# A four-layer graph network on one core: constants of the radial filter loaded first, the first group's node work moved ahead of the edge compaction, and more turns for the last groups' convolutions in the closing steps

## The chip, the cores and the metric

The kernel runs on one core of one Trainium2 chip. The metric is the time of one execution on the device in microseconds. The kernel before took 1791.55 us, the median of three runs between 1784.43 and 1791.74 us. The profiled execution took 1791.61 us, and its page counts a span of 1789.7 us.

## What is computed

128 graphs of 64 nodes with 128 channels go through four layers. Each layer adds a graph operator to x and normalises the result over the channels. Cut to what matters here:

```python
# layer 0: continuous filter, 20 Gaussians of the distance, cosine cutoff at 5
f    = exp(-0.5 / widths**2 * (adj[..., None] - offsets)**2)
W    = (ssp(f @ fw1 + fb1) @ fw2 + fb2) * rcut(adj)[..., None]
agg  = einsum('bjf,bijf->bif', x @ w_in2f, W)
x    = layernorm(x + ssp(agg @ ow1 + ob1) @ ow2 + ob2)
# layer 1: the same form with 64 Gaussians, weighted by adj itself
g    = exp(coeff * (adj[..., None] - offsets1)**2)
Wf   = (ssp(g @ W1.T + b1) @ W2.T + b2) * adj[..., None]**2
y    = einsum('bjf,bijf->bif', x @ Wa.T, Wf)
x    = layernorm(x + ssp(y @ Wd1.T + bd1) @ Wd2.T + bd2)
# layer 2: two graph convolutions with D^-1/2 (A+I) D^-1/2 and elu; layer 3: one, with relu
x    = layernorm(x + gcn2(x, adj))
x    = layernorm(x + relu(norm(adj) @ x @ W.T + b))
```

`ssp` is softplus less log 2. About three quarters of the entries of `adj` are zero, and the kernel works on the nonzero ones only.

## The kernel before, in words

Two graphs make a pair: 128 rows on the 128 partitions, 64 pairs. The program has three parts.

**The opening** (lines 669 to 1674, up to the loop at line 1675). Vector (DVE) counts the edges of each node, and orders the nodes by their number of edges (`count`, `rank`). `permuted(s)` puts the adjacency rows of a set of eight pairs into that order: set 0 by matrix products and one store and two loads over DRAM (line 943, one half on the SP queue and one on the ACT queue), set 1 by eight indirect DMAs of GpSimd (POOL, line 910) and sixteen small loads (line 949). Then the constants of the layers are loaded over the ACT queue (lines 1144 to 1199): `neg_off`, `width` and `coeff` are the offset, the width and the factor of the Gaussians, each loaded in three copies of 20 rows, and Vector works on them (lines 1157 to 1160). `compact(0)` (line 1003) takes the largest entries of each row of set 0 by MAX8, FIND_INDEX8 and MATCH_REPLACE8 (lines 1033 to 1040), after POOL has cleared `comb` and `at` (lines 1017 and 1019); `pack` writes the packed distances d, column numbers j and cutoff weights w to DRAM. After that come a small filter for zero distance (lines 1208 to 1220), `loads(0)` and `loads(1)`, which read d, j and w of the first two pairs over the SP queue (line 1112), `node_before(0, 0)`, which makes the input features of the first group (four transposes, a copy `xt`, an addition on POOL at line 1304, four products, a copy `ys` on Scalar), and the first Gaussians (`gaussians`, line 1514).

**The loop.** 2 x 64 pair visits (layers 0 and 1), three chunks each, and two steps to drain: 386 steps, n and k being visit and chunk of step i. In a step the chunk of this step gets `filter_in` (product `px`, line 1542, and two Scalar passes `h`), the one before gets `gather` (product `pg`, line 1568, with the one-hot matrix `hot`, line 1527), and the one before that gets `filter_out` and `message` (products `pw`, line 1555, and two Vector products `m`, line 1583). After a pair's third chunk `slot_sums` reduces the messages to `agg` (lines 1606 and 1610), three reductions a step. Between these pieces the step gives turns to generators that do everything else: `nodes` (the node work after a group's sums, `node_after`), `befores`, `last`, and the two lanes `convs[0]` and `convs[1]`. A turn is one `next` of a generator, mostly one product into one of two PSUM banks (`ps_n`) or the work that reads it out; `slot` sees to it that a bank filled in one turn is read out in the next call. `graph_convs(q)` is layers 2 and 3 of group q in 29 turns; lane q % 2 takes it.

In layer 1 the groups are 0 to 14 of four pairs each, 15 of two pairs, and 16 and 17 of one pair. Groups 15 to 17 have their own queues in `last`, which get two turns a step. Everything that is still queued after the loop runs in rounds, one turn of each queue a round (the closing rounds).

**The order.** `in_order` ties the instructions of Vector and POOL to program order from the instruction `first` (line 668) to the loop, and those of all engines within the loop and after it. In the opening Scalar, TensorE and the DMA queues are ordered by the framework's scheduler; DMAs of the SP and ACT queues share eight completion semaphores in turn, and a DMA waits until the one before it on its semaphore has landed.

Of the kernel before, what the change touches and what calls it, by code (L numbers as in the profile page):

```python
# [11 lines left out]
F32 = mybir.dt.float32  # L12
AF = mybir.ActivationFunctionType
ALU = mybir.AluOpType
# [4 lines left out]
P = 128  # L19
# [561 lines left out]
def sparse_stack(ctx: ExitStack, tc: tile.TileContext, t: dict, out: bass.AP, flag):  # L581
# [85 lines left out]

    first = nc.cur_bb.bb.instructions[-1]


    places = [const.tile([NB, A], F32, name=f"place{i}") for i in range(2)]

# [3 lines left out]
    def run(queue, n):  # L676

        held = None
        while queue and n:
            try:  # L680
                held = next(queue[0])
                n -= 1
            except StopIteration:
                queue.popleft()
        return held
# [125 lines left out]
    def dram_ap(ap, offset, dims):  # L811
        return bass.AP(tensor=ap.tensor, offset=ap.offset + offset, ap=dims)
# [56 lines left out]
    def part(s):  # L869
        return slice(8 * s, 8 * (s + 1))  # L870

    def load_matrix(name, rows=C):
        w = const.tile([rows, C], F32, name=f"w_{name}")
        nc.scalar.dma_start(w, t[name])
        return w

    def column(name):
        return t[name].rearrange("(p o) -> p o", o=1)

    def load_column(name):  # L880
        b = const.tile([P, 1], F32, name=f"c_{name}")
        nc.scalar.dma_start(b, column(name))
        return b

    def load_terms(name):

        b = const.tile([1, C], F32, name=f"r_{name}")
        nc.scalar.dma_start(b, t[name].rearrange("(o p) -> o p", o=1))
        part_ = const.tile([1, 3, C], BF16, name=f"p_{name}")
        for i in range(3):  # L890
            nc.vector.tensor_copy(part_[:, i, :], b)
            if i < 2:
                nc.vector.tensor_sub(b, b, part_[:, i, :])
        terms = const.tile([3, GS, C], BF16, name=f"t_{name}")
        for s in range(GS):
            nc.scalar.dma_start(terms[:, s, :], part_[0:1].rearrange("o i c -> o (i c)"))
        return terms

    def load_rows(name):
        b = const.tile([P, C], F32, name=f"b_{name}")  # L900
        nc.scalar.dma_start(b, dram_ap(t[name], 0, [[0, P], [1, C]]))
        return b


    def big(name, n=640):
        return cpt.tile([P, 640], F32, tag="big", name=name, bufs=8)[:, 0:n]
# [189 lines left out]
        nc.tensor.matmul(u[0:1, 0:1], lhsT=odds, rhs=one, start=True, stop=True)  # L1096
        nc.vector.tensor_copy(flag, u[0:1, 0:1])

    def loads(n):


        layer, p = divmod(n, NP)
        size = GSLOTS[layer]
        s, at = p // 8, (p % 8) * 2 * size
        assert (layer, s) in stored, "slots are read before they are written"
        d = edge.tile([P, GSLOTS[1]], F32, tag="d", name=f"d_{n}", bufs=3)
        j = edge.tile([P, GSLOTS[1]], BF16, tag="j", name=f"j_{n}")
        w = edge.tile([P, GSLOTS[1]], F32, tag="w", name=f"w_{n}")

        def load(to, name, first, n):  # L1110

            nc.sync.dma_start(to, dram_ap(slots[layer, name][s], first, [[0, to.shape[0]], [1, n]]))  # L1112

        if layer == 0:
            third = 2 * size // 3
            for q in range(3):
                load(d[32 * q : 32 * (q + 1), 0:third], "d", at + q * third, third)
            d = d[0:96, 0:third]
        for b in range(2):
            rows, first = slice(A * b, A * (b + 1)), at + b * size  # L1120
            if layer == 1:
                load(d[rows, 0:size], "d", first, size)
            load(j[rows, 0:size], "j", first, size)
            load(w[rows, 0:size], "w", first, size)
        return d, j, w
# [7 lines left out]
    load_set(0)  # L1133
    permuted_rows, goes, hots = {}, {}, {}
    side, again0 = deque(), []

    goes_to(0)
    run(deque([permuted(0)]), -1)
    for s in (1, 2):
        load_set(s)  # L1140
    run(deque([permuted(1)]), -1)


    neg_off = [const.tile([P, 1], F32, name=f"neg_off{i}") for i in range(2)]
    coeff0 = const.tile([P, 1], F32, name="coeff0")
    width0 = const.tile([P, 1], F32, name="width0")

    fw1 = const.tile([P, C], F32, name="fw1")
    nc.gpsimd.memset(fw1, 0.0)
    nc.vector.memset(neg_off[0], 0.0)  # L1150
    nc.vector.memset(width0, 1.0)
    for q in range(3):
        at = slice(32 * q, 32 * q + NG0)
        nc.scalar.dma_start(fw1[at, :], t["L0_gnn_fw1"])
        nc.scalar.dma_start(width0[at, :], column("L0_gnn_widths"))
        nc.scalar.dma_start(neg_off[0][at, :], column("L0_gnn_offsets"))
    nc.vector.tensor_mul(width0, width0, width0)
    nc.vector.reciprocal(coeff0, width0)
    nc.vector.tensor_scalar(coeff0, coeff0, -0.5, None, ALU.mult)
    nc.vector.tensor_scalar(neg_off[0], neg_off[0], -1.0, None, ALU.mult)  # L1160

    off1 = offsets1()
    width1 = np.float32(off1[1] - off1[0])
# [35 lines left out]
    g["b0"], g["b1"] = load_column("L2_gnn_b0"), load_column("L2_gnn_b1")  # L1199
    g["b2"] = load_rows("L2_gnn_b2")  # L1200
    g["W3"] = load_matrix("L3_gnn_WT")
    g["b3"] = load_terms("L3_gnn_b")
    run(deque([compact(0)]), -1)

    w = layers[0]
    g0 = const.tile([P, 1], F32, name="g0")
    nc.vector.memset(g0, 0.0)
    act(g0[0:32], g0[0:32], AF.Square, bias=neg_off[0][0:32])  # L1210
    act(g0[0:32], g0[0:32], AF.Exp, scale=coeff0[0:32])
    u = ps_n.tile([P, 512], F32, tag="n", name="zero_x")
    nc.tensor.matmul(u[:, 0:1], lhsT=fw1[0:32, :], rhs=g0[0:32], start=True, stop=True)
    h0 = const.tile([P, 1], F32, name="h0")
    act(h0, u[:, 0:1], AF.Exp, bias=w["b1"])
    act(h0, h0, AF.Ln, scale=0.5, bias=half)
    u = ps_n.tile([P, 512], F32, tag="n", name="zero_w")
    nc.tensor.matmul(u[:, 0:1], lhsT=w["w2"], rhs=h0, start=True, stop=True)
    zero_filter = const.tile([P, 1], F32, name="zero_filter")
    nc.vector.tensor_add(zero_filter, u[:, 0:1], w["b2"])  # L1220

    def late_constants():


        eye = const.tile([P, A], F32, name="eye")
        nc.vector.tensor_add(eye, ident[:, 0:A], ident[:, A : 2 * A])
        deg = const.tile([P, NP], F32, name="deg")
        for s in range(NS):
            part_ = a_all[:, part(s), 0:A]
            yield from wait_steps(PACE - 2)  # L1230
            nc.vector.tensor_add(part_, part_, eye.unsqueeze(1).to_broadcast([P, 8, A]))
            yield
            nc.vector.tensor_reduce(deg[:, part(s)], part_, AX.X, ALU.add)
            yield
        g["dinv2"] = const.tile([P, NP], F32, name="dinv2")
        g["dinv3"] = const.tile([P, NP], F32, name="dinv3")
        some = const.tile([P, NP], F32, name="some")

        nc.vector.tensor_scalar(some, deg, 0.0, None, ALU.is_gt)
        nc.vector.tensor_scalar(g["dinv2"], deg, TINY, None, ALU.max)  # L1240
        nc.vector.tensor_scalar(g["dinv3"], deg, GCN_EPS, None, ALU.add)
        for i in (2, 3):
            dinv = g[f"dinv{i}"]
            for s in range(NS):
                yield from wait_steps(PACE)
                nc.gpsimd.tensor_tensor(dinv[:, part(s)], dinv[:, part(s)], neg_half[:, 0:8], ALU.pow)
        yield from wait_steps(PACE)
        nc.vector.tensor_mul(g["dinv2"], g["dinv2"], some)

# [39 lines left out]
    def node_before(layer, q):  # L1291

        w = layers[layer]
        name = f"{layer}_{q}"
        xs = x_all[:, GROUPS[layer][q], :]
        n = xs.shape[1]
        flat, ps = bank(f"xT_{name}", n)
        for s in range(n):
            nc.tensor.transpose(ps[:, s, :], xs[:, s, :], ident)
        yield True  # L1300
        xt = node.tile([P, 512], F32, tag="xt", name=f"xt_{name}", bufs=1)[:, 0 : n * P]
        nc.vector.tensor_copy(xt, flat)

        nc.gpsimd.tensor_tensor(xs, xs, w["c2"].unsqueeze(1).to_broadcast([P, n, C]), ALU.add)
        yield
        flat, ps = bank(f"y_{name}", n)
        for s in range(n):
            nc.tensor.matmul(  # L1308
                ps[:, s, :], lhsT=xt[:, s * P : (s + 1) * P], rhs=w["win"], start=True, stop=True
            )  # L1310
        yield True
        y = node.tile([P, n, C], F32, tag=f"y{n}", name=f"ys_{name}", bufs={GS: 3, 2: 1, 1: 2}[n])
        act(y, ps, AF.Copy)
        feats[layer, q] = y
        yield

    zblk = const.tile([P, GS, P], F32, name="zblk")
    nc.gpsimd.memset(zblk, 0.0)
# [318 lines left out]
        yield from late_constants()  # L1637

    N = 2 * NP
    for n in range(2):  # L1640
        slot_data[n] = loads(n)
    run(deque([node_before(0, 0)]), -1)
    gaussians(0, 0)
    gaussians(0, 1)
    one_hot(0)
# [29 lines left out]
    for i in range(3 * N + 2):  # L1675
# [15 lines left out]
        if n < N:  # L1691
# [14 lines left out]
                    one_hot(n)  # L1706
            filter_in(c)
        slot(nodes)
        if k == 1 and befores:
            slot(befores)  # L1710
        for queue in last:
# [66 lines left out]
```

## Time and profile before

| part of the span | what the profile shows |
|---|---|
| 0 to 78 us | the opening; TensorE has 9.3 us of work in the first 80 us, Vector 54.5 us |
| 78 to 1728 us | the loop; TensorE and Vector both near nine tenths busy |
| 1728 to 1783 us | the closing rounds |
| whole span | TensorE 1574.4 us busy (88%), Vector 1568.2 (88%), Scalar 1402.2 (78%), POOL 622.7 (35%) |

A line of the timeline has the start in us, the duration, the engine (a `q` after its name is its queue of DMAs), the line of the kernel, the operation, what it writes and reads, and in brackets how long the engine had been idle and what ended that. A line of the stretches view has the start and end of a stretch, its length, then the busy time of TensorE, of its weight loads, of Vector, Scalar and POOL with the number of instructions, then the granted share of the TensorE clock and the use of DMA.

### The profile page before, as it was taken

To read this page: it belongs to the slowest core of one execution; us is meant where nothing else is said; L and a number is where in the kernel's file an instruction comes from. 1 tells how busy PE (TensorE), PEld (TensorE's weight loads), DVE (VectorE), ACT (ScalarE), POOL (GpSimd) and SP (SyncE) were. 2 spreads that over 40 slices of the span, in tenths; PEclk is the share of its full clock that TensorE was granted. 3 is DMA by queue.
4 is the path that set the end of the run, shared out by engine and by line. 5 is a ranking of instruction groups with operands and counts; after the bars stand their busy time and mean duration, and the time that the engine had idled before them with its cause. 6 is when DMAs were issued, how large, how long until landed. Compare 5 with 4: busy or idle time off the path is not lost.

```text
span 1789.7 us, 23999 instructions
## 1 busy us (share of the span) xinstructions
PE 1574.4 (88%) x6806; PEld 786.9 (44%) x6806; DVE 1568.2 (88%) x4457; ACT 1402.2 (78%) x1680; POOL 622.7 (35%) x934
## 2 busy tenths in 40 slices
PE   1298989898989998999999999999999999999975
PEld 1133434444444444444444445454454544545443
DVE  7599989999989998879788999899998898988984
ACT  1277878788878887888999888888888888888840
POOL 2134353525333233214312333234242243332345
PEclk9999999999989998999999999999999999999995
DMA  5354545455445444534655655555555555545400
GB/s 140 89 121 120 148 128 129 112 123 130 120 117 124 104 119 105 128 97 119 148 135 123 143 122 122 136 118 128 123 134 126 119 123 132 125 118 132 96 7 15
DMA packets 123463, 210.12 MB, mean 117 GB/s; under 512 B 44709, under 2 KB 71478, under 8 KB 123318
## 3 DMA queue, kind: packets, MB, share of 16 engines
q1 hardware_dynamic: 114112, 202.18, 47.5%
q0 software_dynamic: 4352, 5.02, 1.0%
q10 hardware_dynamic: 4854, 1.27, 0.3%
q8 instruction: 56, 0.92, 0.2%
q14 instruction: 89, 0.73, 0.2%
HBM read 195.87 MB, written 12.51 MB: 116 GB/s over the span
## 4 chain that ended last, share of the span: by engine, by line
PE 43%; DVE 31%; DMA 7%; ACT 6%; issue 6%; SPq 3%; POOL 3%; DVEq 0%; ACTq 0%; POOLq 0%
PE pw L1555 16%; PE pg L1568 8%; PE px L1542 7%; DVE m L1583 6%; DVE agg L1606 6%; DVE hot L1527 5%; ACT h L830 2%; DMA cb<-code_dram 2%; SPq L1112 2%; DVE st L1276 2%; DMA d<-d_dram 2%; DVE mv L1277 2%; ACT g L830 2%; PE y L1308 1%; PE o L1387 1%
## 5 line engine op out<-in xcount | busy, mean ns | idle before, releaser
L830 ACT ACTIVATE g<-pg 128x728 f32<-128x728 f32 (+1 forms) x384 | 313.0, 815 | 163.4 <-PE pg L1568 156.7
L830 ACT ACTIVATE h<-h,half 128x728 f32<-128x728 f32 (+2 forms) x385 | 364.6, 947 | 12.5
L1568 PE MATMUL pg<-hot,ys 64*128 64x364 f32 (+1 forms) x1536 | 363.8, 551 | 0.1
L1606 DVE TENSOR_REDUCE agg<-m 128x16 f32<-128x288 f32 (+9 forms) x896 | 342.3, 430 | 2.1
L1281 POOL TENSOR_TENSOR rs<-rs,neg_half 128x4 f32<-128x4 f32 (+2 forms) x70 | 68.7, 981 | 736.6 <-DVE rs L1279 730.6
L1555 PE MATMUL pw<-h,w_L_gnn_fw 128*128 128x364 f32 x768 | 294.7, 509 | 31.7 <-DVE m L1583 31.7
L1555 PE MATMUL pw<-h,w_L_gnn_W2T 128*128 128x420 f32 x768 | 315.5, 533 | 3.2 <-DVE m L1583 3.2
L1583 DVE SCALAR_TENSOR_TENSOR m<-pw,c_L_gnn_b,g 128x420 f32<-128x420 f32 x384 | 239.9, 650 | 50.9 <-PE pw L1555 35.1
L1583 DVE SCALAR_TENSOR_TENSOR m<-pw,c_L_gnn_fb,g 128x364 f32<-128x364 f32 x384 | 212.1, 589 | 39.9 <-PE pw L1555 36.3
L830 ACT ACTIVATE h<-px,c_L_gnn_b 128x840 f32<-128x840 f32 x192 | 183.5, 956 | 60.2 <-PE px L1542 60.2
L1568 PEld LDWEIGHTS pg<-hot,ys 64*128 64x128 f32 x1536 | 118.2, 189 | 192.9 <-ACT h L830 107.3
L1555 PEld LDWEIGHTS pw<-h,w_L_gnn_fw 128*128 128x128 f32 x768 | 138.0, 198 | 137.8 <-DVE m L1583 73.7
L1555 PEld LDWEIGHTS pw<-h,w_L_gnn_W2T 128*128 128x128 f32 x768 | 130.6, 190 | 140.7 <-issue 76.2
L1527 DVE SCALAR_TENSOR_TENSOR hot<-j,row,w 128x1092 f32<-128x1092 bf16 (+1 forms) x128 | 183.4, 1432 | 5.1 <-DMA w<-w_dram 5.1
L1542 PE MATMUL px<-d,fw 32*128 32x364 f32 x768 | 173.0, 527 | 14.5 <-ACT h L830 12.1
L830 ACT ACTIVATE h<-px,c_L_gnn_fb 128x728 f32<-128x728 f32 x192 | 165.8, 864 | 11.2 <-PE px L1542 7.3
L1542 PE MATMUL px<-d,w1t 64*128 64x420 f32 x768 | 174.4, 531 | 0.0
L830 ACT ACTIVATE d<-d,neg_off 96x728 f32<-96x728 f32 (+1 forms) x128 | 141.8, 1108 | 0.0
L910 POOL DMA_INDIRECT rows<-comb,goes x64 | 68.4, 1069 | 141.7 <-DMA rows<-comb,goes 90.5
L1542 PEld LDWEIGHTS px<-d,fw 32*128 32x128 f32 x768 | 58.7, 186 | 117.0 <-ACT h L830 49.4
L1283 POOL TENSOR_SCALAR x_all<-ny,mv,rs 128x128 f32<-128x128 f32 x128 | 100.8, 797 | 3.6
L1542 PEld LDWEIGHTS px<-d,w1t 64*128 64x128 f32 x768 | 68.5, 186 | 53.3 <-issue 38.2
(219 smaller groups left out, 2135.0 us busy)
## 6 DMA issues: line engine op xcount, KB each, us to landing
d<-d_dram SPq DMA_DIRECT2D x128, 315.0 KB
w<-w_dram SPq DMA_DIRECT2D x128, 315.0 KB
w<-w_dram SPq DMA_DIRECT2D x128, 273.0 KB
j<-j_dram SPq DMA_DIRECT2D x128, 157.5 KB
d<-d_dram SPq DMA_DIRECT2D x192, 91.0 KB
j<-j_dram SPq DMA_DIRECT2D x128, 136.5 KB
x_all<-in_x_dram SPq DMA_DIRECT2D x8, 512.0 KB
cb<-code_dram SPq DMA_DIRECT2D x31, 128.0 KB
```

What stands on the lines that cost most here:

```text
L830: latest = nc.scalar.activation(out_, in_, func, **kw)
L910: nc.gpsimd.indirect_dma_start(out=into, out_offset=bass.IndirectOffsetOnAxis(ap=at, axis=0), in_=rows, in_offset=None,)
L1112: nc.sync.dma_start(to, dram_ap(slots[layer, name][s], first, [[0, to.shape[0]], [1, n]]))
L1276: nc.vector.bn_stats(stats[:, s, :], y[:, s, :])
L1281: nc.gpsimd.tensor_tensor(rstd, rstd, neg_half[:, 0:n], ALU.pow)
L1283: nc.gpsimd.tensor_scalar(dst[:, s, :], y[:, s, :], mv[:, s, 0:1], rstd[:, s : s + 1], ALU.subtract, ALU.mult,)
L1527: nc.vector.scalar_tensor_tensor(hots[n][:, 0:size], j[:, 0:size], near, wt[:, 0:size], ALU.is_equal, ALU.mult)
L1542: nc.tensor.matmul(ps[:, b, 0:n], lhsT=w["w1"][rows, :], rhs=d[rows, col : col + n], start=True, stop=True,)
L1555: nc.tensor.matmul(ps[:, 0 : c["size"]], lhsT=c["w"]["w2"], rhs=c["h"][:, b, :], start=True, stop=True)
L1568: nc.tensor.matmul(ps[:, b, 0:n], lhsT=y[rows, :], rhs=hots[c["n"]][rows, at], start=True, stop=True,)
L1583: nc.vector.scalar_tensor_tensor(messages[n][:, b, at], c["pw"][b][:, 0:size], c["w"]["b2"], c["g"][:, b, :], ALU.add, ALU.mult,)
L1606: nc.vector.tensor_reduce(av[:, :, :, r], both, AX.X, ALU.add)
```

## The change

The changed kernel has three edits. It moves what the Gaussians need (`neg_off`, `coeff`, `width`, `fw1`) from behind `permuted(1)` to directly behind `first`, so that their loads and the Vector work on them come first. It puts the other constants' loads ahead of `goes_to(0)`, moves the zero filter and `node_before(0, 0)` ahead of `compact(0)`, issues the three d loads of the first pair from the ACT queue, and takes `load_terms` (a bias in three bf16 terms, five small Vector operations and four DMAs) into the late constants inside the loop. And in the last steps (i of 372 and above) each step gives one more turn to each of the two lanes of convolutions, so that groups 12, 13 and 14 get further before the closing rounds.

```diff
+    neg_off = [const.tile([P, 1], F32, name=f"neg_off{i}") for i in range(2)]
+    coeff0 = const.tile([P, 1], F32, name="coeff0")
+    width0 = const.tile([P, 1], F32, name="width0")
+
+    fw1 = const.tile([P, C], F32, name="fw1")
+    nc.gpsimd.memset(fw1, 0.0)
+    nc.vector.memset(neg_off[0], 0.0)
+    nc.vector.memset(width0, 1.0)
+    for q in range(3):
+        at = slice(32 * q, 32 * q + NG0)
+        nc.scalar.dma_start(fw1[at, :], t["L0_gnn_fw1"])
+        nc.scalar.dma_start(width0[at, :], column("L0_gnn_widths"))
+        nc.scalar.dma_start(neg_off[0][at, :], column("L0_gnn_offsets"))
+    nc.vector.tensor_mul(width0, width0, width0)
+    nc.vector.reciprocal(coeff0, width0)
+    nc.vector.tensor_scalar(coeff0, coeff0, -0.5, None, ALU.mult)
+    nc.vector.tensor_scalar(neg_off[0], neg_off[0], -1.0, None, ALU.mult)
...
-    def loads(n):
+    def loads(n, engine=nc.sync):
...
-            nc.sync.dma_start(to, dram_ap(slots[layer, name][s], first, [[0, to.shape[0]], [1, n]]))
+            (engine if name == "d" else nc.sync).dma_start(to, dram_ap(slots[layer, name][s], first, [[0, to.shape[0]], [1, n]]))
...
-    goes_to(0)
-    run(deque([permuted(0)]), -1)
-    for s in (1, 2):
-        load_set(s)
-    run(deque([permuted(1)]), -1)
...
-    g["b3"] = load_terms("L3_gnn_b")
-    run(deque([compact(0)]), -1)
-
+    goes_to(0)
+    run(deque([permuted(0)]), -1)
+    for s in (1, 2):
+        load_set(s)
+    run(deque([permuted(1)]), -1)
...
     nc.tensor.matmul(u[:, 0:1], lhsT=w["w2"], rhs=h0, start=True, stop=True)
+
+    run(deque([node_before(0, 0)]), -1)
+    run(deque([compact(0)]), -1)
     zero_filter = const.tile([P, 1], F32, name="zero_filter")
...
     def late_constants():
 
+        yield from load_terms("L3_gnn_b")
...
-    for n in range(2):
-        slot_data[n] = loads(n)
-    run(deque([node_before(0, 0)]), -1)
+    slot_data[0] = loads(0, nc.scalar)
+    slot_data[1] = loads(1)
...
         slot(nodes)
+        if i >= 3 * (N - GS):
+
+            slot(convs[0])
+            slot(convs[1])
         if k == 1 and befores:
```

The helpers `load_matrix`, `column`, `load_column`, `load_terms`, `load_rows`, and `bank` to `node_before`, move with them; `load_terms` becomes a generator and issues its four DMAs from the SP queue.

## The prediction

> **What bounds the kernel now.** I read the stretches first, to see which engine the loop, its last steps and the closing rounds wait for; then Vector's waits in the first 100 us; then the opening in the timeline, with the chain of waits for the landings; then the closing rounds in the timeline.
>
> Stretches (start and end, length, busy time and number of instructions of TensorE, its weight loads, Vector, Scalar and POOL, granted clock, DMA share, GB/s): steady loop, the last 14 steps, the closing rounds.
>
> ```profile
> 1600.00:1660.00 60.00, 58.10 (x261) 30.04 (x260) 54.32 (x129) 52.50 (x60) 21.62 (x27) 1.00 0.57 132
> 1660.00:1728.00 68.00, 61.59 (x266) 31.28 (x265) 59.96 (x137) 49.45 (x61) 26.36 (x34) 0.99 0.21 49
> 1728.00:1784.00 56.00, 34.01 (x150) 25.62 (x148) 36.26 (x127) 5.31 (x15) 31.93 (x48) 0.68 0.05 14
> ```
>
> TensorE is 97% busy in the steady loop, 91% in the last 14 steps (Vector 88%), and 61% in the closing rounds, where the clock falls. So nothing in the steady loop is for sale; the change can act on the opening, on those 14 steps, and on the closing rounds.
>
> Vector's longest wait in the first 100 us, and the opening around it:
>
> ```profile
> DVE neg_off L1160 <- DMA neg_off<-in_L_gnn_offsets_dram: 8.7, 1, 8.7
> ```
>
> ```profile
> 4.72 0.69 DVE L770 TENSOR_SCALAR within<-entries 128x1024 bf16<-128x1024 f32 x1 [1.81 <-DMA entries<-in_adj_dram]
> ...
> 11.24 1.23 DVE L697 TENSOR_TENSOR halves<-some 128x2048 bf16<-128x2048 bf16 x1
> ...
> 39.88 0.69 SPq L943 DMA_DIRECT2D ad<-perm  x1
> ...
> 43.84 0.96 POOL L910 DMA_INDIRECT perm<-a_all,index  x1 [0.30 <-issue]
> ...
> 46.14 0.65 ACTq L943 DMA_DIRECT2D ad<-perm  x1
> ...
> 49.22 0.15 DVE L1160 TENSOR_SCALAR neg_off<-neg_off 128x1 f32<-128x1 f32 x1 [8.69 <-DMA neg_off<-in_L_gnn_offsets_dram]
> ...
> 51.78 1.11 DVE L1033 MAX8 comb<-ad 128x8 f32<-128x64 f32 x8
> ...
> 75.36 1.27 POOL L1304 TENSOR_TENSOR x_all<-x_all,b_L_gnn_ob 128x512 f32<-128x512 f32 x1 [4.43 <-PE xT L1299]
> ...
> 78.17 0.60 ACT L830 ACTIVATE ys<-y 128x512 f32<-128x512 f32 x1 [4.49 <-PE y L1308]
> 78.67 0.89 ACT L830 ACTIVATE d<-d,neg_off 96x728 f32<-96x728 f32 x1
> ...
> 80.54 1.58 PE L1542 MATMUL px<-d,fw 32*128 32x364 f32 x4 [2.40 <-ACT d L830]
> ```
>
> The ACT queue holds, in order, three loads of `fw1`, the second half of `ad`, and the last `neg_off`. The first waits for the memset of `fw1`, which stands on POOL behind eight indirect DMAs (the last from 43.84). So half of `ad` leaves at 46.14, though SP's half left at 39.88, and Vector stands until 49.22. At the other end of the opening, `ys` is on Scalar ahead of the first Gaussians.
>
> The chain of waits (start, duration, what) shows what a load costs here, among the entries' megabytes and in quiet:
>
> ```profile
> 1.38 4.78 DMA b<-in_L_gnn_fb_dram
> 6.18 3.70 DMA entries<-in_adj_dram
> ...
> 46.83 2.29 DMA neg_off<-in_L_gnn_offsets_dram
> ```
>
> The closing rounds:
>
> ```profile
> 1727.19 0.65 DVE L1583 SCALAR_TENSOR_TENSOR m<-pw,c_L_gnn_b,g 128x420 f32<-128x420 f32 x1 [0.35 <-PE pw L1555]
> ...
> 1734.99 0.49 PE L1367 MATMUL u<-agg,w_L_gnn_Wd1T 128*128 128x128 f32 x2 [3.44 <-DVE gz L1506]
> ...
> 1746.63 1.93 PE L1456 MATMUL hw<-w_L_gnn_W,er 128*128 128x128 f32 x8 [0.95 <-DVE er L1414]
> ```
>
> After the last `m` (end 1727.84) the last pair, group 17, still needs its node work and its 29 turns; its `u` starts at 1734.99, behind reductions and groups 13 and 14.
>
> [...] 4.78 us for a bias among the entries, 2.29 us for `neg_off` in quiet. [...] the 8.69 us at line 1160 hold the compaction queued behind it. [...] 0.68 granted in the closing rounds, and the eight products `hw` there take 1.93 us against 1.16 us in the loop (at 1701.65).
>
> **The change part by part.**
>
> *Constants first.* The built order of the changed kernel puts Vector's work on `width0`, `coeff0` and `neg_off` at the head, ahead of the counting, which Vector starts at 4.72 now. It waits for six small loads. The third `width` load is held until the load of `w` has landed (3.05), the third `neg_off` load until the bias `b` has (1.38 + 4.78 = 6.16); it then lands after 2.29 us in quiet (8.5) or 3.7 us behind an entries load (9.9). I take 3.0: 9.2. Behind this wait on Vector is all of the counting. From there: 0.15 for `neg_off`, about 0.8 of small work now done before 4.7, then four pairs of passes at 0.645 us each pass without gaps, 5.15. `halves` starts at 15.3 instead of 11.24: Δ = 4.0 (3.3 to 4.7; 2.6 if the load is back by 7.9). Scalar's `below` pass and the other constants' loads lie beside this.
>
> What it buys: `fw1` is no longer between the halves of `ad`, so both leave at about 39.9 + Δ and land some 3 us later. But POOL's order is now eight indirect DMAs (end 44.8 + Δ), the addition on `x_all` (1.27), the memset of `comb` (0.39): the first MAX8 can start at 46.5 + Δ. Gain: 51.78 − 46.5 − 4.0 = 1.3 us (0.6 to 2.7). The terms of the bias (1.2 us on Vector, 49.29 to 50.55) are within this; in the loop they are five short instructions among 386 steps, and I count nothing: they can go into the 10% that Vector idles.
>
> *Node work and zero filter ahead of compaction; d over the ACT queue.* Scalar ends the cosine at 70.47, loads a table (1.28) until 71.8, and can issue the d loads at once, where SP issued them at 72.71: 0.9 us. Landing 3.2 us after issue, as now (72.71 to 75.88), at 75.0. Then two Gaussian passes (0.9 each): `px` at 76.9 instead of 80.54, 3.6 us sooner, for `xT`, `y` and `ys` are done by then. Not all of it stays: the second d load and the first `hot` (ready about 82 on this scale) hold the steps after. I take 2.8 (2.0 to 3.6). The node work itself, 1.1 + 0.7 + 2.1 + 0.6 us on three engines, lies in the 40 us in which TensorE does next to nothing; the addition on POOL is counted above.
>
> Opening: −1.3 − 2.8 ≈ −4 (−2 to −5.5).
>
> *Two more turns a step.* In the built order 13 of Vector's instructions move from behind the last `m` to before it: group 13's end (`gy_sup` 0.69, `gz` 0.60, four statistics with their aggregates and `rs`, 1.7) and five turns of group 14 (`er` 0.6, `gy_hw` 0.6): 4.2 us. On TensorE group 13's `sup` 1.1 and `o` 1.4 and group 14's `hw` 1.1: 3.6; on POOL 4.5, which has room. If the 14 steps keep TensorE at 61.6/68 busy, they grow by 3.6/0.906 = 4.0; by Vector's measure 4.2/0.88 = 4.8. I take 4.4. From both sides: nothing, if the turns go into the 6.4 and 8 us of idle time; 7.5 if I walk through the new order with today's durations, because earlier turns put products right behind the Vector work they read: group 13's `gh` behind `gxt`, which is behind a `hot` (2.5), group 14's `u` behind its sums (1), group 15's `u` behind two groups' statistics (3), with 1 us more of small ones.
>
> What the closing rounds give back: group 17's chain sets their end, and the removed work is only partly on it. Its `u` starts 7.15 us after the last `m` now and would at 6.3, for a statistics block of group 13 stands ahead of it; after that fewer turns share the engines for the first rounds. The walk gives 53.6 us from the last `m` to the last normalisation against 55.5: −2 (−0.5 to −5; 5 would be all the moved work of TensorE at half clock, 1.7 + 1.6 + 1.6).
>
> End: +4.4 − 2 = +2.4. Whole: −4 + 2.4 = −1.6: 1790 us.
>
> **The rivals.**
>
> A, both ends fill: the moved turns cost nothing in the 14 steps, since the stretch before them shows that 97% can be had, the rounds give all 5 back, and the opening gives 5.5: 1791.55 − 10.5 = 1781. Against it: in these steps Vector too is at 88%, and in-order queues make waits of added turns.
>
> B, the last steps stall: the walk is right, +7.5, the rounds return only 0.5, the opening 2: +5, 1797 us, slower. For it: the wait of 3.44 us at group 17's `u` shows such a wait behind a reduction already. Against: the walk adds up waits that the real order may overlap.
>
> C, the wait moves from the middle to the head: each late `neg_off` load queues behind a megabyte, comes at 12 to 13, Δ reaches 7.5, and the first MAX8 comes 2.2 later than now; with 2.8 back at the end of the opening this leaves −0.6 of the 4: with +2.4, 1793 us, slower by little. For it: the bias of 4.78 us. Against: the entries are gone by 9.9.
>
> **How the numbers follow.** Forecast 0.52, A 0.25, B 0.16, C 0.07. The predicted time is the forecast's 1790. The range reaches to A and B with a little more for the runs' own spread (7 us between the three before): 1778 to 1799. Faster by over 0.5% is below 1782.6: most of A and the forecast's lower edge, 0.24. Slower by over 0.5% is above 1800.5: B's edge, and a spread that falls badly, 0.12. The rest, 0.64, cannot be told from no change.
>
> **What would show it right or wrong.** Right: Vector's wait at its head ends at about 9.2 and `halves` starts near 15.3; the first MAX8 starts near 50.5, released by the memset of `comb` on POOL; the first `px` near 75.6 instead of 80.54; from there the loop runs as now to step 372; the 14 steps from the first of them to the last `m` take some 4 us more, with TensorE's added idle time behind `gxt`, `agg` or the statistics; from the last `m` to the end some 2 us less. Wrong: a head wait over 12 us; a first step that starts early but is given back by a later wait for d, j or the edges; 14 steps of the same length or over 6 us longer; closing rounds that fall by 5, or not at all.

## The result, and the profile after

The changed kernel takes 1799.42 us (median, 1797.76 to 1801.56), the kernel before 1790.25 us in the same comparison (1784.43 to 1791.74). The ratio is 1.0058, 95% interval 1.0032 to 1.0084: slower by 9 to 10 us, where 1790 us were predicted. The profiled executions differ by 6.1 us (spans 1795.8 and 1789.7 us), and the traces show where.

To find the place I read from each trace the end of certain message products (the 768 instructions that write `m`, two a step): the first, the 385th (start of layer 1), the 737th (step 370, just ahead of the last steps) and the last one.

| end of message product, us | before | after | difference |
|---|---|---|---|
| 1st | 91.10 | 87.18 | −3.92 |
| 385th | 870.10 | 862.08 | −8.02 |
| 737th | 1656.46 | 1648.44 | −8.02 |
| 768th, the last | 1727.85 | 1734.54 | +6.69 |
| end of the span | 1789.7 | 1795.8 | +6.1 |

The changed kernel is 4 us ahead when the loop begins and 8 us when its last steps begin; those lose 14.7 us, and the closing rounds return 0.6. In what follows, "last steps" is the stretch from the end of the 737th message product to the end of the last one, and "closing rounds" the stretch from there to the end.

**The opening.** Vector's waits in the first 100 us, and the timeline of the changed kernel:

```profile
DVE hot L1531 <- DMA w<-w_dram: 8.9, 1, 8.9
DVE width L719 <- DMA width<-in_L_gnn_widths_dram: 6.1, 1, 6.1
...
DVE neg_off L722 <- DMA c_L_gnn_fb<-in_L_gnn_fb_dram: 2.5, 1, 2.5
```

```profile
10.14 0.15 DVE L722 TENSOR_SCALAR neg_off<-neg_off 128x1 f32<-128x1 f32 x1 [2.47 <-DMA c_L_gnn_fb<-in_L_gnn_fb_dram]
...
15.70 1.23 DVE L751 TENSOR_TENSOR halves<-some 128x2048 bf16<-128x2048 bf16 x1
...
51.54 1.11 DVE L1055 MAX8 comb<-ad 128x8 f32<-128x64 f32 x8 [1.87 <-POOL comb L1039]
...
76.58 1.65 PE L1546 MATMUL px<-d,fw 32*128 32x364 f32 x4 [29.03 <-ACT d L884]
```

The wait of 8.7 us for `neg_off` in the middle is gone; two waits at Vector's head (6.1 and 2.5 us) have come, until 10.14. `halves` starts 4.5 us later than before, yet the first MAX8 0.2 us sooner and the first `px` 4.0 us sooner (80.54 before). The MAX8 is released by POOL's memset of `comb`. For the second wait at the head the profile names a load that `neg_off` doesn't read; what the operation needs by the code is its own last load, issued at 6.20, 3.9 us before. (Such a wait of one load for the landing of another is in the trace of before: SP's last load of `entries` stood 4.1 us until the ACT queue's `b` had landed, which it doesn't read.) The longest wait in the list, of the first `hot` for its weights w, ends at 80.20 (81.13 before); the product `pg`, which reads `hot`, starts at 81.75.

**The last steps and the closing rounds.** The two stretches, the kernel before first, then the changed one.

```profile
1656.46:1727.85 71.39, 64.98 (x281) 32.53 (x278) 63.11 (x150) 52.95 (x65) 28.60 (x36) 0.99 0.25 58
1727.85:1789.72 61.87, 34.16 (x150) 25.77 (x149) 36.41 (x127) 5.31 (x15) 31.93 (x48) 0.67 0.05 15
```

```profile
1648.44:1734.54 86.10, 71.73 (x305) 36.88 (x301) 68.26 (x163) 53.05 (x65) 37.48 (x41) 0.94 0.22 51
1734.54:1795.84 61.30, 29.78 (x125) 22.02 (x124) 32.48 (x114) 5.20 (x15) 26.82 (x43) 0.66 0.04 11
```

TensorE gets 6.75 us more busy time. By the prediction's count 3.6 of them are the moved products; the rest, about 3 us, is my estimate for the lower granted clock (0.94 against 0.99). Its idle time grows from 71.39 − 64.98 = 6.4 us to 86.10 − 71.73 = 14.4. What TensorE waits for in that stretch, before and after (total, times, longest):

```profile
PE u L1367 <- DVE agg L1610: 3.7, 2, 2.6
PE back L1396 <- DVE gxt L1469: 1.1, 1, 1.1
```

```profile
PE u L1371 <- DVE agg L1614: 6.0, 3, 3.6
PE gh L1477 <- DVE gxt L1473: 4.6, 2, 2.6
PE y L1263 <- DVE nh L1379: 1.5, 1, 1.5
```

Not all of these waits are new. The three of `u` in the changed kernel are those of groups 14 (1.10 us), 15 (3.58) and 16 (1.32); before, group 14's was 1.04, group 15's nothing and group 16's 2.62. `y` doesn't read `nh`. By the code it takes the PSUM bank of `u`, which `nh` reads out, so that wait is for a bank.

The product `gh` of group 13 in the kernel before, then the first of the new waits in the timeline of the changed kernel, and the piece of the stretch in which that `gh` runs:

```profile
1664.37 1.12 PE L1473 MATMUL gh<-gxt,w_L_gnn_W 128*128 128x512 f32 x2 [0.23 <-DVE gxt L1469]
```

```profile
1654.17 1.52 DVE L1531 SCALAR_TENSOR_TENSOR hot<-j,row,w 128x1260 f32<-128x1260 bf16 x1
...
1655.61 0.69 DVE L1473 COPY gxt<-gx 128x512 f32<-128x512 f32 x1
...
1656.35 2.08 PE L1477 MATMUL gh<-gxt,w_L_gnn_W 128*128 128x512 f32 x2 [2.60 <-DVE gxt L1473]
...
1658.21 2.06 PE L1559 MATMUL pw<-h,w_L_gnn_W2T 128*128 128x420 f32 x4
1659.68 1.29 DVE L1587 SCALAR_TENSOR_TENSOR m<-pw,c_L_gnn_b,g 128x420 f32<-128x420 f32 x2 [2.79 <-PE pw L1559]
```

```profile
1655.78:1659.19 3.41, 2.84 (x4) 1.45 (x5) 1.11 (x2) 0.68 (x1) 3.02 (x4) 0.50 0.63 149
```

The product `gh` of group 13 waits 2.60 us for its copy `gxt`, which is behind `hot` on Vector. `pw`, queued behind `gh`, comes late, and then Vector stands 2.79 us for `pw`. `gh` takes 2.08 us, where the same product took 1.12 before: the granted clock is 0.50 there. In the last steps the trace has the clock at 1.00 except for three such pieces of 3.41 us (from 1655.78, 1720.63 and 1730.87); before, only the final 1.56 us of the stretch lie in one. Each of the three begins during or within 1 us after a wait of TensorE (2.60, 2.04 and 1.32 us). The longest wait, 3.58 us until 1712.11, is followed by none.

### The profile page after: what moved, and what is told of

It is laid out like the page before. It is cut to its first block, busy times and chain, and to the rows that moved or that the text cites. A ratio compares the mean times of both kernels' runs of the same rounds, so it can differ in the third digit from the quotient of the medians.

```text
span 1795.8 us, 24007 instructions
## 1 busy us (share of the span) xinstructions
PE 1572.4 (88%) x6806; PEld 787.1 (44%) x6806; DVE 1569.0 (87%) x4457; ACT 1402.2 (78%) x1681; POOL 624.6 (35%) x934
## 4 chain that ended last, share of the span: by engine, by line
PE 42%; DVE 34%; DMA 7%; ACT 7%; issue 5%; SPq 3%; POOL 2%; DVEq 0%; ACTq 0%; POOLq 0%
PE pw L1559 15%; PE pg L1572 8%; DVE m L1587 7%; PE px L1546 7%; DVE agg L1610 6%; DVE hot L1531 5%; ACT h L884 2%; SPq L1134 2%; DVE st L1231 2%; DVE mv L1232 2%; DMA d<-d_dram 2%; ACT g L884 2%; DMA cb<-code_dram 2%; DVE at L1058 1%; PE o L1391 1%
## 5 line engine op out<-in xcount | busy, mean ns | idle before, releaser
L884 ACT ACTIVATE h<-px,c_L_gnn_b 128x840 f32<-128x840 f32 x192 | 183.4, 955 | 58.5 <-PE px L1546 58.5
```

What stands on the lines that cost most here:

```text
L884: latest = nc.scalar.activation(out_, in_, func, **kw)
```

## The experiments

The kernels below ran on four chips, each time together with the kernel before, whose median there was 1792.4, 1802.8, 1802.2 and 1790.9 us in turn; so across chips only ratios to the kernel before are compared. Each stretch comes from one profiled execution. From the 385th to the 737th message product nearly every kernel below takes 786.3 to 786.4 us (one takes 785.1), so what is before and after it can be read apart.

**Each end of the change alone.** `open_only` is the changed kernel without these lines, `end_only` the kernel before with them:

```diff
         slot(nodes)
+        if i >= 3 * (N - GS):
+            slot(convs[0])
+            slot(convs[1])
```

> The changed kernel without the extra turns in the last steps. The traces show the changed kernel 3.9 us ahead after the first message product and 8.0 us ahead before the last steps. Theory 1 (the opening is a real gain, and the last steps alone lose): the last 14 steps and the closing rounds are as in the kernel before, so 1790.25 - 8.0 = 1782 us. Rival (only the 4 us of the opening are caused by the change, the other 4 are chance of one execution): 1786 us. The prediction on record put the opening at -4: 1786 us.

> The kernel before with the two extra turns a step alone. Theory 1 (the loss is in the last steps and has nothing to do with the opening): 71.4 us from the first of the last steps to the last message product become 86 us, the closing rounds give 0.6 back: 1790.25 + 14 = 1804 us. The prediction on record, taken alone: +2.4, 1793 us. Rival (the loss needs the changed opening, by another phase of the queues): at most 1795 us.

Measured: `open_only` 0.9986 of before (0.9976 to 0.9997), 2.5 us less by the ratio; `end_only` 1.0098 (1.0074 to 1.0122), 17.5 us more. The last steps of `open_only`, then of `end_only`:

```profile
1651.34:1723.52 72.18, 65.77 (x280) 32.84 (x278) 63.11 (x149) 52.92 (x65) 28.52 (x36) 0.98 0.25 57
```

```profile
1653.42:1740.02 86.60, 71.59 (x304) 36.71 (x301) 68.33 (x162) 52.92 (x65) 37.66 (x41) 0.94 0.22 51
```

So the loss is the third edit's alone and needs nothing of the opening.

The opening gains some 2 to 6 us up to layer 1 in single profiles; the 8 us of the first profile were partly chance. Kernels on the same chip show it: the 385th message product ended at 867.0 us with the old opening (`end_only`) and at 865.0 and 865.2 with the new one; on the second chip at 878.5 with the old one and at 873.3 and 873.9 with the new; on the third at 878.3 and 878.5 with the old one and at 872.4 with the new. The 1782 us of theory 1 failed; 2.5 us are nearer to the 4 of its rival and of the prediction, which the interval just includes.

**Place.** The same turns at the end of the step, or at its head ahead of `hot`:

```diff
         run(side, 1)
+        if i >= 3 * (N - GS):        # turns_at_step_head
+            slot(convs[0])
+            slot(convs[1])
...
         for queue in last:
             slot(queue)
+        if i >= 3 * (N - GS):        # turns_at_step_end
+            slot(convs[0])
+            slot(convs[1])
         past = [c, c1]
```

> The changed kernel with the same two extra turns in the same steps, moved from behind the node turn (ahead of filter_out) to the end of the step. Theory P (place: the turns put a convolution product right behind the Vector copy it reads and ahead of the ready products pw, so TensorE stands with pw queued behind it): no wait of gh on gxt of 2.6 us in these steps, they grow by about 5 us instead of 14.7, total 1782 + 5 = 1787 us (1784 to 1791). Theory W (amount: there is no room on Vector and TensorE in these steps, wherever the turns stand): 1799 us, as the changed kernel.

> The changed opening with both extra turns at the head of the step, before the one-hot matrix is put on Vector's queue. It takes away the cause of the longest single wait of the changed kernel (product gh of group 13 behind the copy gxt, which stands behind hot, 2.6 us) without taking a turn away. Theory C (turns there cost wherever they stand, since Vector and TensorE wait for each other in turn): that wait goes and others come, the last steps still take 84 to 89 us. Rival (this one order is bad): at most 80 us.

Measured: 1.0088 (1.0071 to 1.0105) at the end, 1.0034 (1.0020 to 1.0048) at the head; last steps 88.6 and 86.4 us. My theory of the place fell: at the end of the step the wait of `gh` shrinks (1.0 us in all), but `u` waits 10.8 us for `agg`, and `sup` 3.4 for `nTs`. At the head `gxt` does stand ahead of `hot`, and `gh` still waits 2.21 us for it, behind messages and sums on a Vector that is never idle there.

**Number.** One turn more, for the lane of group 13 only:

```diff
         slot(nodes)
+        if i >= 3 * (N - GS):
+            slot(convs[1])
```

> The changed opening with one extra turn a step instead of two, for the lane of group 13 only, at the same place. Theory C (each turn that is moved into the last steps costs there, in proportion): about half of the extra: the last steps take 72.2 + 7 = 79 us instead of 86, the whole is 7 us above the run without extra turns, about 1797 us. Rival (there is room for some turns, and only the second one a step overfills the steps): at most 2 us above that run, 1792 us. Rival (the first moved turn already brings the stalls, the second adds nothing): 86 us in the last steps, 1804 us.

Measured: 1.0077 (1.0049 to 1.0104); last steps 91.1 us, at a clock of 0.88. Half the turns cost about as much as both, so the loss is not in proportion to them. (Part of the 91.1 is the clock, by my estimate: TensorE is busy 75.1 us there, against 71.7 at a clock of 0.94 in the changed kernel, and idles 16.0 against 14.4.)

**The amount of work without its links.** On the opening of `open_vector_later` (below):

```diff
+        twice = c["n"] >= 2 * NP - GS and c["k"] == 0
-        for b in range(2):
+        for b in (0, 1, 0, 1) if twice else (0, 1):      # px made twice
...
         slot(nodes)
+        if i >= 3 * (N - GS) and i % 2 == 0:
+            nc.vector.tensor_reduce(scrap, zblk.rearrange("p s c -> p (s c)"), AX.X, ALU.add)
```

> The opening of the run with Vector's operations moved back, no extra turns; in the last 14 steps the amount of work that the change moves is added without its links: the product px is made twice in the four steps with the first chunk of a pair (4 x 0.9 us on TensorE; the result is the same), and Vector gets seven reductions of a constant 128x512 tile (some 0.6 us each, 4 us) that nobody waits for. Theory A (amount: these steps have no room): the last steps take about 86 us as with the extra turns. Theory L (links: a product that reads what Vector has just been told to write is what costs, the amount alone fits or costs its share): 72.5 us grow by 0 to 5 us, and the whole by as much.

Measured: 0.9985 (0.9967 to 1.0002). The stretch of the last steps, first of the control `open_vector_later`, then of this kernel:

```profile
1651.18:1723.64 72.46, 66.05 (x282) 33.03 (x279) 63.10 (x150) 52.93 (x65) 28.53 (x36) 0.98 0.24 57
```

```profile
1658.10:1730.94 72.84, 67.36 (x299) 33.91 (x296) 67.33 (x156) 53.01 (x65) 28.57 (x36) 1.00 0.24 56
```

Vector does 4.2 us more and TensorE 16 instructions more (each doubled `px` takes 1.6 to 1.7 us instead of 0.9 to 1.0, so some 2.8 us in all, where the moved products are 3.6), and the stretch grows by 0.4 us. The clock flatters this a little: it was 1.00 here and 0.98 in the control. Against `closing_without_14` below, whose last steps took 71.0 us at a clock of 1.00, the growth is 1.8 us. That is still far from 14.7. So the amount fits, nearly, into the idle time of these steps. What costs is that the moved products are links of a chain, each behind something that Vector has only just been told to do. The run does not tell a wait for an operand from a wait for a PSUM bank, nor from the changed order of the turns themselves; POOL's 8.9 us of added work are not in it either, but no wait of TensorE or Vector in the changed kernel's last steps names POOL.

**Another engine for the links.** The copies out of PSUM for groups 12 to 14 on Scalar:

```diff
+            if q in (12, 13, 14):
+                act(y, ps, AF.Copy)              # gy_hw, gy_sup; likewise gxt
+            else:
                 nc.vector.tensor_copy(y, ps)
```

> The changed kernel, extra turns included, but for groups 12, 13 and 14 the copies out of PSUM in layers 2 and 3 (gxt, gy_hw, gy_sup) are made by Scalar instead of Vector. Theory L (the waits come from Vector's queue, in which these copies stand behind the one-hot matrix, the messages and the sums): the waits of gh for gxt go, the sums come sooner, and the last steps take 76 to 82 us instead of 86. Rival (any queue does it; Scalar's passes h, g and d stand before the copies in its own queue): 85 to 90 us.

Measured: 1.0040 (1.0014 to 1.0067), last steps 86.5 us. The rival holds. The timeline of this kernel:

```profile
1663.80 0.99 ACT L884 ACTIVATE h<-h,half 128x840 f32<-128x840 f32 x1
...
1664.70 0.58 ACT L884 ACTIVATE gxt<-gx 128x512 f32<-128x512 f32 x1
...
1665.43 1.42 PE L1483 MATMUL gh<-gxt,w_L_gnn_W 128*128 128x512 f32 x2 [2.10 <-DVE nTs L1453]
...
1674.15 1.16 PE L1513 MATMUL o<-w_L_gnn_WT,gy_sup 128*128 128x128 f32 x8 [1.70 <-ACT gy_sup L884]
```

`gxt` now stands behind Scalar's pass `h` and ends at 1665.28, at the same moment as Vector's `nTs`, which the profile names, though `gh` reads `gxt` and not `nTs`; `gh` stalls for 2.10 us (2.60 in the changed kernel), and `o` for 1.70 on `gy_sup` from Scalar. The three `u` still wait 6.1 us for their sums, which stay on Vector. These links are late on either queue.

**The opposite.** No turns for the lanes in the last 7 steps, opening as in `open_vector_later`:

```diff
-        if convs[0]:
+        if convs[0] and i < 3 * (N - GS) + 7:
             slot(convs[0])
...
-        slot(convs[1])
+        if i < 3 * (N - GS) + 7:
+            slot(convs[1])
```

> The opposite of the change's third edit, on the opening of the run with Vector's operations moved back: in the last 7 of the 14 last steps the two lanes get no turn at all. Theory G with theory C (a convolution turn in the last steps costs more than its work, since it couples TensorE and Vector there, and the closing rounds give such work a place beside group 17's chain): the time from the first of the last steps to the last message product falls from 72.4 us to 64 to 68 us, and the closing rounds (62.7 us) grow by at most 2 us: 4 us below the run with the same opening. Rival (what is taken from the loop comes back in the closing rounds at least in full, at a lower clock): no gain, or up to 5 us slower.

Measured: 0.9977 (0.9964 to 0.9989), the same as with that opening alone. The last steps fall to 65.3 us, but the closing rounds grow from 62.7 to 74.3: the rival holds. Less in the last steps is paid back in full.

**What the closing rounds are worth.** After the loop, lanes are emptied and their work left out:

```diff
     run(sums, -1)
+    convs[0].clear()        # group 14
+    convs[1].clear()        # group 13
     while nodes or convs[0] or convs[1] or any(last):
```

> The kernel before; after the loop the two lanes of convolutions are emptied, so that what is left of groups 13 and 14 in layers 2 and 3 (and their output) is left out. It is the most that any number of extra turns could take out of the closing rounds. Theory G (the closing rounds are the chain of the last pair, group 17, and the work of groups 13 and 14 lies beside it): from the last message product to the end 58 to 62 us instead of 61.9, the whole within 4 us of before. Rival (the closing rounds are bound by the amount of work on the engines): the rounds lose the share of work removed, about a third, some 20 us, and the whole is about 1770 us. The prediction on record counted 2 us (0.5 to 5) for the part that the change moves.

> The kernel before, after the loop the lane of group 14 is emptied: what is left of group 14 in layers 2 and 3, and its output, is left out. With both groups left out the closing rounds took 45.9 us instead of 61.9. Theory K (group 14 takes a turn in nearly every round beside the last pair's chain, and its normalisations stand on POOL before the last pair's): the rounds take 47 to 50 us. Rival (the two groups share it evenly by their work): 52 to 55 us.

> The kernel before, after the loop the lane of group 13 is emptied: the rest of group 13 (its last products, its last normalisation, its output) is left out, which is most of what the change moves into the loop. Theory K (in the first rounds the last pair waits for its own sums, so that this work is nearly free there): the closing rounds take 60 to 62 us. Rival (they are bound by the work on the engines): 54 to 57 us. The prediction on record counted 2 us for it: 60 us.

Measured for the whole: 0.9909 (0.9878 to 0.9940) without both, 0.9935 (0.9906 to 0.9965) without 14, 0.9997 (0.9983 to 1.0011) without 13. The closing rounds without group 14, and without group 13:

```profile
1735.78:1783.68 47.90, 25.76 (x90) 17.79 (x89) 26.17 (x98) 4.68 (x14) 21.97 (x36) 0.56 0.05 14
```

```profile
1736.32:1797.68 61.36, 33.72 (x141) 25.46 (x140) 34.22 (x117) 5.32 (x15) 27.38 (x43) 0.64 0.04 11
```

Theory G, on which this part of the prediction rested, fell: the rounds are not group 17's chain alone, for 16 us of the 61.9 go with both groups (45.9 left). But it is group 14 that costs 14 us. Group 13, all of which the change moves away, costs 0.5 us in this profile, at a clock of 0.64 against 0.67, and the ratio of the whole leaves it at about 3 us or less.

**Why five turns of group 14 returned nothing.** In the closing rounds of the changed kernel:

```profile
1753.86 3.12 POOL L1238 TENSOR_SCALAR x_all<-gz,mv,rs 128x128 f32<-128x128 f32 x4
...
1757.62 0.80 POOL L1238 TENSOR_SCALAR x_all<-ny,mv,rs 128x128 f32<-128x128 f32 x1
...
1758.47 0.47 PE L1470 MATMUL gx<-ident,x_all 128*128 128x128 f32 x1 [2.83 <-POOL x_all L1238]
```

Group 14's normalisation stands right ahead of group 17's on POOL. Before, it came after it (1755.24 behind 1747.92). One edit takes group 14's normalisations off POOL:

```diff
         for s in range(n):
-            nc.gpsimd.tensor_scalar(
+            (nc.vector if name in ("2_14", "3_14") else nc.gpsimd).tensor_scalar(
```

> The changed kernel, but group 14's two normalisations in layers 2 and 3 (each four passes of 0.8 us on POOL) are made by Vector. In the changed kernel the first of them stands on POOL directly ahead of the last pair's first normalisation, and TensorE waits 2.8 us for that. Theory Q (this order on POOL took what the five moved turns of group 14 would have given back): the closing rounds fall from 61.3 us at a granted clock of 0.66 to 56 to 58.5. Rival (those turns lay beside the last pair's chain, which waits for something else then): 60 to 62 us. The last 14 steps stay at 86 us in both.

Measured: 1.0037 (1.0023 to 1.0052). The closing rounds take 58.7 us at a clock of 0.62, where those of the changed kernel and of `end_only` took 61.3 (0.66) and 64.6 (0.58), some 63 between them; `gx` waits 0.5 us instead of 2.8. That is about 4 us less; 58.7 lies just above the expected 56 to 58.5, and below the rival's 60. It supports the reading, and two runs above agree with it. In `turns_at_step_head` group 14's normalisation comes after group 17's on POOL itself (1768.88 behind 1766.35), and the closing rounds took 58.1 us at 0.62; in `turns_at_step_end` it stands ahead (1761.37, then 1765.13), and they took 64.9 at 0.61.

The last steps took 89.3 us, not 86:

```profile
1650.87:1740.15 89.28, 74.90 (x305) 38.59 (x301) 68.24 (x162) 53.06 (x65) 37.43 (x41) 0.90 0.21 49
```

The edit changes nothing there: the waits of TensorE are those of the changed kernel to 0.1 us, and its idle time is the same 14.4 us. Only its busy time is 3.2 us longer, at a clock of 0.90 instead of 0.94. So the clock's part of the loss differs by that much between two executions with the same stalls.

**Versions.** `open_vector_later` keeps the changed opening, but puts the four small Vector operations behind the permutation, and gives no extra turns. Two more start from it.

```diff
     run(deque([permuted(1)]), -1)
+    nc.vector.tensor_mul(width0, width0, width0)
+    nc.vector.reciprocal(coeff0, width0)
+    nc.vector.tensor_scalar(coeff0, coeff0, -0.5, None, ALU.mult)
+    nc.vector.tensor_scalar(neg_off[0], neg_off[0], -1.0, None, ALU.mult)
```

> The changed opening, no extra turns, the loads of the Gaussians' constants still first, but the four small Vector operations on them (width squared, reciprocal, two scalings) moved back behind the permutation, so that the counting does not stand behind the loads. Theory 1 (the head wait costs the opening its 4.5 us): Vector's halves start at 11.2 instead of 15.7, the first MAX8 at about 47 instead of 51.5, the first px at about 72.1 instead of 76.6, total 4.5 us below the run without extra turns, about 1777.5 us. Rival (a later wait for d, w or the edges of the next set takes the gain back): the same time as without extra turns, 1782 us.

> The same opening, no extra turns; in the closing rounds the lane of group 14 is passed over in every third round while the small groups have turns left. Group 14 ends some 12 us before the last pair, and costs the rounds 14 us. Theory K (group 14's turns delay the last pair's chain turn by turn): of its 28 turns some 9 move behind, at up to 0.5 us each: the closing rounds fall from 62.7 us to 58 to 61. Rival (group 14 then ends last, or the order of the queues meets new waits): 62 us or more.

> A version after what the runs show: the opening with Vector's operations moved back, no extra turns, and the normalisations of groups 14, 16 and 17 on Vector instead of POOL, since Vector is busy only 36 of 62 us in the closing rounds and a pass of 128x128 takes POOL 0.8 us. Theory Q: the closing rounds lose the POOL passes of the last pair's chain (three of 0.8 us, less some 0.3 us each on Vector) and the waits behind group 14's: 62.7 us become 56 to 60, the whole is 3 to 6 us below the run with the same opening, about 0.995 of before. Rival (Vector's queue then holds the chain up as POOL's did): the same 62 to 63 us.

```diff
+            if queue is convs[0] and rounds % 3 == 0 and any(last):   # open_lane_two_of_three
+                continue
             slot(queue)
...
+            (nc.vector if name in ("2_14", "3_14", "1_16", ..., "3_17") else nc.gpsimd).tensor_scalar(   # open_norms_on_vector
```

Measured: `open_vector_later` 0.9979 (0.9966 to 0.9992), 3.8 us less than before by the ratio. It was expected 4.5 us below `open_only`; the medians show 0.7, and the intervals overlap. Its first MAX8 starts at 48.30 and its first `px` at 73.37, 3.2 us ahead of the changed kernel, but at the 385th message product it is level with `open_only` (864.8 and 865.0): layer 0 takes the gain back in that pair of profiles. `open_lane_two_of_three` 0.9979 (0.9966 to 0.9991): nothing. `open_norms_on_vector` 0.9959 (0.9940 to 0.9977), 1781.73 against 1790.85 us: the lowest ratio of all kernels here that compute everything, faster than both. Its closing rounds took 63.4 us at a clock of 0.55, where `open_only` had 65.2 and `amount_without_turns` 64.4 at the same clock: 1 to 2 us less, where 56 to 60 us in all were expected. The rest of its profile's lead is made in layer 0 (385th message product at 855.1 us, 863.1 in `open_lane_two_of_three` on the same chip), so its lead over `open_vector_later`, whose interval overlaps, is not settled.

## Why the prediction was wrong

*Constants first: mechanism right, sizes near.* The head wait ended at 10.14 instead of 9.2 (the last load took 3.9 us, where 3.0 were taken, an estimate between 2.29 and 3.7; what sets the time of a small load the traces do not show), `halves` started at 15.70 instead of 15.3 (Δ 4.5 instead of 4.0), and the first MAX8 stood behind POOL's memset of `comb`, as said: it gained 0.2 us where 1.3 stood in the sum. Of the 1.1 us missing Δ took 0.5, and one of POOL's indirect DMAs, which lasted 1.65 us instead of 0.96, the rest.

*Node work and d: right, and a little better.* From the first MAX8 to the first `px` 28.8 us became 25.0, a gain of 3.7 where 2.8 (to 3.6) stood. Together 4.0 at the first `px`, as forecast; 2 to 6 us are left at layer 1 in single profiles, and 2.5 in the ratio of `open_only`. The two parts of this edit, the earlier node work and the d loads from the ACT queue, were not run apart.

*Two more turns: the step that failed is "I take 4.4".* It priced the moved turns by the share of busy time of the 14 steps. Measured: 14.7 us, twice the upper bound of 7.5: 8.0 us of added idle time of TensorE, 3.6 of moved products and about 3 that I estimate for the lower clock. The text had the mechanism at hand, as rival B, and gave it 0.16. The walk through the new order named `gh` behind `gxt` and `hot` (2.5; measured 2.60, against 0.23 before) and group 15's `u` (3; measured 3.58, against none). These came as walked. Group 14's `u` behind its sums (1; measured 1.10) was no new wait, for it was 1.04 before. What the walk lacked:
- two more stalls, `gh` for `gxt` once more (2.04) and `y` for the PSUM bank that `nh` reads out (1.52); against them, group 16's `u` waits 1.3 us less than before, and `back` no longer waits 1.1 us for `gxt`;
- that the granted clock is lower in these steps, 0.94 instead of 0.99. The busy time grows by 6.75 us for 3.6 us of moved products: some 3 us that no step of the prediction counted. The prediction counted a lower clock for the closing rounds only (before, 0.68 over the rounds and 0.50 from 1760 to 1780 us); the changed kernel's trace has 0.50 in the loop too, where `gh` takes 2.08 us against 1.12. That the stalls bring it about is argued from where these pieces lie, not shown: over the kernels here more idle time does not always go with a lower clock (17.1 us at 0.95 in `turns_at_step_end`, 12.9 at 0.92 in `turns_at_step_head`).

The argument of rival A, that idle time absorbs work, holds for work without links (0.4 us, or 1.8 at an equal clock, for about the same amount), not for links.

*Closing rounds: −2 forecast, −0.6 measured,* within the stated 0.5 to 5, but less than the 3 us by which equal closing rounds differ between profiles. The detail was right (group 17's `u` starts 6.0 us after the last `m` instead of 7.1; forecast 6.3), but what that gained was lost again on POOL, to group 14's normalisation, as far as the three runs above show it. That group 13's end is worth only 0.5 us there, and group 14's work 14, was the fact to look for.

*Sum.* With −4 for the opening, +14.7 and −0.6 the steps give 1791.55 + 10 = 1802, against 1799.4 measured. Of the rivals, B had the mechanism, the closing rounds (0.5), and about half of the size (7.5 of 14.7). C had the direction, slower, but not the cause: the head wait ended at 10.1, nearer to the forecast's 9.2 than to C's 12 to 13, and the opening gained.

What stays open: what decides where a piece at a granted clock of 0.50 falls, how the loss divides between operands, PSUM banks and the order of the turns, and why layer 0 gives back more in one run than in another.

## What to carry to other kernels

Price work that is moved into a nearly full in-order loop by its links, not by its busy time: for each moved product ask what it reads, how far back in the other engine's queue that stands, and what is queued behind. Here a walk through the new order that found stalls by name came nearer than the estimate from utilisation. And before moving work out of a tail, leave it out once: here one group was worth 0.5 us in its profile and its neighbour 14.

## What the runs showed that was not expected

- About the same amount of work, unlinked, in steps with TensorE at 91% and Vector at 88%, cost 0.4 us of 72.5.
- One extra turn a step cost about as much as two (last steps 91.1 us, against 86.1, 86.6 and 89.3 in three kernels with two).
- The same instructions with the same stalls took 86.1 and 89.3 us, at granted clocks of 0.94 and 0.90.
- Equal closing rounds took 61.9, 62.7 and 65.2 us at granted clocks of 0.67, 0.63 and 0.55 in three kernels that do the same work there: some 3 us of a run's spread are made in the last 60.
